# Padding the rows that expert lists gather from 260 to 272 numbers, in a graph-attention and mixture-of-experts kernel

## The chip, the core and the metric

The kernel runs on one core of one Trainium2 chip. The metric is the device time of one execution in microseconds (us); lower is better. The engines are PE (TensorE, matmuls; its weight loads are shown as PEld), DVE (VectorE), ACT (ScalarE), POOL (GpSimd) and SP (SyncE, which here only issues DMAs). Data moves by DMA between the device memory and the on-chip memory (128 partitions); matmul results land in PSUM.

## What is computed

One layer over 3327 nodes of 256 numbers: a graph attention over a sparse adjacency matrix, then a mixture of 16 experts, of which each node uses two.

```python
# graph attention, 4 heads of 64
h = (layernorm(x) @ W).reshape(n, 4, 64)
e = leaky_relu(einsum('nhd,d->nh', h, a1 + a2), 0.2)        # one score per node and head
attn = softmax(where(adj[:, None, :] > 0, e[:, :, None], -9e15), axis=-1)
x = x + layernorm(einsum('nhm,mhd->nhd', attn, h).reshape(n, 256)) * gamma + beta

# experts
xn = layernorm(x)
probs = softmax(xn @ gate_w + gate_b)
top_probs, top_idx = top_k(probs, 2); top_probs /= sum(top_probs)
hidden = silu(xn @ w1[e]) * (xn @ w2[e])                    # for every expert e
x = x + sum over the two chosen e of top_prob_e * (hidden @ w3[e])
```

## The kernel before

**Tiles and groups.** The 3327 nodes are padded to 26 tiles of 128. The tiles form seven groups (`SIZES`, line 68: 4, 4, 4, 4, 3, 4, 3). A group's rows lie on chip in one of the tiles of `XF` (line 259), 128 partitions by tiles of the group by `ROW` numbers, of which `X` is the first 256.

**Attention.** The adjacency matrix is loaded a group by a group at a time (L614), turned into a mask of zeros and ones by DVE (L617), and multiplied on PE with the nodes' values, split into a high and a low part (L640, L641). After each of the seven steps over rows, `finish` (line 664) turns a group's sums into its new rows: scaling by heads, two normalisations, the gate's logits, the choice of two experts.

**What is gathered later.** For each node `finish` makes a row of `ROW = D + 4 = 260` numbers in the tile `pay`: 256 normalised values (L765), two weights (L826, L827), and the numbers of the two experts (`chosen`, line 813; L816 writes the numbers, L817 and L819 make masks of them). SP stores a group's rows into the table `normed` in device memory (line 357, issued at L890). `places` (L833 to L837, PE) counts each node's place in its experts' lists, `placed`, `hot_rows`, `hot_pieces` (DVE), `coded` (ACT) and `listing` (PE, L874) write the lists.

**The experts.** There are 19 lists: experts 0 to 2 have an early list each, taken from groups 0 to 4 once these are done (`early_lists`, line 923), and a second one; the other 13 experts have one each, sorted by length (`all_lists`, line 935). `take_list` (line 1195) works a list off: 
- POOL gathers the rows of 128 nodes at a time from `normed` (`gather`, L1022; 61 instructions in all) into one of three buffers `XE`, which are the tiles `XF[0]`, `XF[1]` and `XF[5]`, free by then. Each indirect DMA reads whole rows of `ROW` numbers. Three lists' rows can thus be on chip or on their way at a time. 
- The rows are transposed, on PE (L1226) for lists 0 to 7 and by DMA transposes (L1180) for later ones. 
- The products with `w1` and `w2` (L1037 for lists 0 to 5; for later ones L1098, with seven products in place of eight, made by sums of blocks on DVE, L1070, and by copies between PSUM banks on ACT and DVE, L1104 and L1108), the gate (L1130, L1250) and the products with `w3` (L1151). 
- `weigh` (line 1025) picks each row's weight for this expert from its last four numbers (L1028, L1030). The results are scaled (L1274, L1276) and added into `out` by POOL's indirect DMAs (L1154).

**What sets the order.** From the first load to the last scatter-add, every piece of work is an entry in a `Plan` (class at the top of the kernel): engine, cost in us, rank, what it comes after, buffers. `best_order` tries 340 orders, in which the works of `finish` get small random delays; it simulates each with the entries' costs and sizes, and emits the one with the least simulated end. The emitted order is the order of each engine's queue. `chosen` is entered with a cost of 0.75 (`cho`, line 879), and the store with `size=n * P * ROW * 4` (L890).

**Constants.** At the start POOL fills tables, and clears what follows the 256 values in the three gather buffers (L352).

A few lines that the change touches:

```python
XF = [const.tile([P, len(tiles), ROW], F32, name=f"x{g}") for g, tiles in enumerate(GROUPS)]   # 259
XE = [XF[0], XF[1], XF[5]]                                                                     # 261
for xe in XE:                                                                                  # 351
    nc.gpsimd.memset(xe[:, :, D:], 0.0)
normed = tc.dram_tile([NP, ROW], F32, name="normed")                                           # 357
"pay": lambda key: work.tile([P, GT, ROW], F32, name="pay"),                                   # 421
```

Of the kernel before, what the change touches and what calls it, by code (L numbers as in the profile page):

```python
# [48 lines left out]
F32 = mybir.dt.float32  # L49
# [6 lines left out]
P = 128  # L56
# [3 lines left out]
D = 256  # L60
# [9 lines left out]
GROUPS = [list(range(sum(SIZES[:g]), sum(SIZES[:g + 1]))) for g in range(len(SIZES))]  # L70
# [21 lines left out]
PARTS = {m: 4 if m <= P // 4 else 2 if m <= P // 2 else 1 for m in range(1, P + 1)}  # L92

AGAIN = 2
ROW = D + 4
NONE = float(1 << 20)
I32 = mybir.dt.int32
U32 = mybir.dt.uint32
# [154 lines left out]
def gnn_moe(ctx: ExitStack, tc: tile.TileContext, x, adj_t, W, a, gamma, beta, gate_w, gate_b, w1, w2, w3, out):  # L253
    nc = tc.nc

    const = ctx.enter_context(tc.tile_pool(name="const", bufs=1))


    XF = [const.tile([P, len(tiles), ROW], F32, name=f"x{g}") for g, tiles in enumerate(GROUPS)]
    X = [t[:, :, :D] for t in XF]  # L260
    XE = [XF[0], XF[1], XF[5]]

# [93 lines left out]
    first_w3 = const.tile([P, JC * D], F32, name="first_w3")  # L356
    normed = tc.dram_tile([NP, ROW], F32, name="normed")

    WE = {}

    def load_weights(tiles, e, behind=()):

        at = bass.ds(e, 1)
        first = nc.sync.dma_start(tiles[0], w1[at].rearrange("o (k p) h -> p (o k) h", p=P))
        for other in behind:
            tc.add_manual_dep(first.ins, other.ins.name, mybir.DependencyInfo(
                mybir.DependencyClass.Sync, mybir.DependencyReason.DATA), reason="weights come behind these rows")
        nc.sync.dma_start(tiles[1], w2[at].rearrange("o (k p) h -> p (o k) h", p=P))
        nc.sync.dma_start(tiles[2], w3[at].rearrange("o (j p) d -> p (o j) d", p=P))

    def weight_tiles():
        up = POOLS["wmore"].tile([P, 2, KC, HID], F32, name="w12e")
        return [up[:, 0], up[:, 1], POOLS["wmore"].tile([P, JC, D], F32, name="w3e"), up]
# [13 lines left out]
    PE, DVE, ACT, POOL, SP = "PE", "DVE", "ACT", "POOL", "SP"  # L387
# [19 lines left out]
    def few_h(key):  # L407
# [12 lines left out]
        "w": lambda key: weight_tiles(),  # L420
        "pay": lambda key: work.tile([P, GT, ROW], F32, name="pay"),
        "xt": lambda key: work.tile([P, GT, KC, P], F32, name="xt"),
# [26 lines left out]
    plan = Plan(SLOTS, take)  # L449
# [10 lines left out]
    def by_tile(ap):  # L460
        return ap.rearrange("(t p) d -> p t d", p=P)
# [202 lines left out]
    def finish(g, terms, added, tables):  # L664
        tiles = GROUPS[g]
        n = len(tiles)
        late = int(g > EARLY_GROUP)
        ak, hk, pk, xk, ck = ("agg", g), ("hp", g), ("pay", g), ("xt", g), ("hc", g)
        rank = (3, g)

        fk = ("few", g)
# [7 lines left out]
        def pay():  # L679
            return T[pk]  # L680
# [4 lines left out]
        def some(name):  # L685
            return T[fk][name]
# [121 lines left out]
        def largest(t):  # L808
            best, who = some("best"), some("who")
            nc.vector.max(best[:, t, :], some("lg")[:, t, :])  # L810
            nc.vector.max_index(who[:, t, :], best[:, t, :], some("lg")[:, t, :])

        def chosen():
            names = pay()[:, :n, D + 2:D + 4]
            hot, both = some("hot"), some("both")
            nc.vector.tensor_copy(names, some("who")[:, :, :2])  # L816
            nc.vector.tensor_tensor(hot, number[:, None, None, :].to_broadcast([P, n, 2, NE]),  # L817
                                    names[:, :, :, None].to_broadcast([P, n, 2, NE]), op=ALU.is_equal)
            nc.vector.tensor_add(both, hot[:, :, 0, :], hot[:, :, 1, :])  # L819
# [51 lines left out]
        def listing():  # L871
# [4 lines left out]
        lk, ik = ("ph", "place", g), ("ph", "list", g)  # L876
        w = plan.add(DVE, 0.48, rank, gated + [root], biased, [gk, fk])
        top = [plan.add(DVE, 0.43, rank, [w], lambda t=t: largest(t), [fk]) for t in range(n)]
        cho = plan.add(DVE, 0.75, rank, top, chosen, [pk, fk])
        w = plan.add(DVE, 0.15, rank, top, lambda: nc.vector.tensor_sub(  # L880
            gap()[:, 0], some("best")[:, :, 1], some("best")[:, :, 0]), [fk])

# [2 lines left out]
        else:  # L885
# [4 lines left out]
        stored = plan.add(SP, 0.4, (2, g), [wei, cho] + xn, lambda: nc.sync.dma_start(  # L890
            by_tile(normed[tiles[0] * P:(tiles[-1] + 1) * P, :]), pay()[:, :n, :]), [pk], landing=1.8, size=n * P * ROW * 4)
        pla = plan.add(PE, 0.2, (0, g), [cho] + tables, places, [lk, fk], slack=slack)
# [132 lines left out]
    def weigh(weight, xe, tiles, name):  # L1025

        hit = small.tile([P, CT, 2], F32, name="hit")
        nc.vector.scalar_tensor_tensor(hit[:, :tiles], xe[:, :tiles, D + 2:], name, xe[:, :tiles, D:D + 2],  # L1028
                                       op0=ALU.is_equal, op1=ALU.mult)
        nc.vector.tensor_reduce(weight[:, :tiles], hit[:, :tiles], AX.X, ALU.add)  # L1030

# [163 lines left out]
    def take_list(i, indexed, stored, weights, opened, order):  # L1195
# [20 lines left out]
        def weighed():  # L1216
            weigh(T["weight", i], XE[i % 3], len(tiles), expert[:, i:i + 1])
# [97 lines left out]
    for step in range(NG):  # L1315
        if step + 1 < NG:
            g = step + 1
# [13 lines left out]
    for g in range(NG):  # L1331
        if g + 1 < NG:
            for step in range((g + 1) * NG, (g + 2) * NG):
                products(step, adjacency(step))
        s, c, l, d = finish(g, terms, add_beta(g, read[g]), tables)
        stored.append(s)
        spare.append(d)
        tables = [c]
        if g == EARLY_GROUP:
            i, c = early_lists(c, l)  # L1340
            tables = [c]
            ready.update({k: (i, list(stored)) for k in range(EARLY)})
        if g == NG - 1:
            i, ranked, o = all_lists(c, l)
            ready.update({k: (i, list(stored)) for k in range(EARLY, 2 * EARLY)})
            ready.update({k: (o, list(stored)) for k in range(2 * EARLY, NL)})
# [10 lines left out]
    def first_weights():  # L1357

        WE[0] = [at.rearrange("p (k m) -> p k m", k=k) for at, k in zip(
            [XF[g].rearrange("p t d -> p (t d)")[:, :KC * HID] for g in (2, 3)] + [first_w3], (KC, KC, JC))]  # L1360
        load_weights(WE[0], 0)
# [30 lines left out]
    with tc.If(many["value"] > 0):  # L1392
        with tc.For_i(0, NL) as i:
# [4 lines left out]
            with tc.For_i(0, full * (NT // AGAIN)) as c:  # L1398
# [3 lines left out]
                hit = small.tile([P, AGAIN, 2], F32, name="hit_again")  # L1402
# [7 lines left out]
                n = AGAIN * P  # L1410
# [53 lines left out]
```

## Time and profile before

| | us |
|---|---|
| median of 6 runs (513.77 to 516.5) | 514.48 |
| the profiled execution | 514.71 |
| its span, first to last instruction | 512.9 |
| PE busy | 495.0 |
| DVE busy | 343.9 |
| ACT busy | 247.3 |
| POOL busy | 215.6 |
| POOL in gathers (L1022), 61 instructions | 66.2 |
| POOL in scatter-adds (L1154), 61 instructions | 97.7 |

The mean granted clock of PE is 0.992 of full speed. A span is the time from the first instruction's start to the last one's end; the execution's time has 1.8 us more around it. A stretch's line gives, for each engine, the busy us and the number of instructions, then the granted clock, the mean busy share of the 16 DMA engines, and GB/s moved. A line of the order of time gives the start and the duration in us, the engine, the source line, the operation, and in brackets how long the engine was idle before it and what ended that. A line of waits gives who waited, for whom, us in total, how often, and the longest.

The gather's DMA queue (q0) also carries the scatter-adds: 13.75 MB of the 100.06 MB that the execution moves.

### The profile page before, as it was taken

The page shows a single profiled execution, that of the slowest core. Times are in us where ns is not written, and L with a number is a line of the kernel's source. Part 1 is how long each engine was busy: PE and PEld are TensorE (multiplying, and loading weights), DVE is VectorE, ACT ScalarE, POOL GpSimd, SP SyncE. Part 2 cuts the span into 40 slices and gives each one's busy share as a digit, 9 for nine tenths or more (in the row PEclk, how much of TensorE's full clock was granted, in tenths as well). Part 3 has the DMA queues.
Part 4 walks back from the last instruction along what each step waited for, and adds up shares of the span by engine and source line. Part 5 has one row for each costly group of instructions (what it writes and reads, how often), then busy time and mean ns, then how long its engine had stood idle before and what let it go on. Part 6 is the DMA issues. An engine that isn't in the chain of part 4 may idle for free. (4 is left out here: it accounts for less than half of the span.)

```text
span 512.9 us, 9578 instructions
## 1 busy us (share of the span) xinstructions
PE 495.0 (97%) x3239; PEld 447.0 (87%) x3240; DVE 343.9 (67%) x992; ACT 247.3 (48%) x679; POOL 215.6 (42%) x235
## 2 busy tenths in 40 slices
PE   8999999999999999999999996999999999999994
PEld 5889999999999999986778785988898999988983
DVE  5977563966859798678926486465567668777320
ACT  2661054456446844465322564555455556445441
POOL 5420021112022121746468665645855474543263
PEclk9999999999999999999999998999999999999998
DMA  8942979789779997474269765787877987682233
GB/s 258 365 159 66 316 239 304 240 276 303 235 248 314 358 333 250 128 262 104 64 154 329 223 140 95 138 167 176 175 129 183 220 238 152 85 251 23 25 41 38
DMA packets 85703, 100.06 MB, mean 195 GB/s; under 512 B 27150, under 2 KB 59154, under 8 KB 85652
## 3 DMA queue, kind: packets, MB, share of 16 engines
q1 hardware_dynamic: 74612, 85.42, 53.3%
q0 software_dynamic: 10768, 13.75, 17.4%
q8 instruction: 26, 0.43, 0.4%
q10 hardware_dynamic: 272, 0.26, 0.1%
q14 instruction: 25, 0.20, 0.1%
HBM read 81.55 MB, written 13.75 MB: 186 GB/s over the span
## 5 line engine op out<-in xcount | busy, mean ns | idle before, releaser
L640 PE MATMUL pa<-hi,mk 128*128 128x258 f32 x676 | 167.9, 289 | 0.0
L641 PE MATMUL pa<-lo,mk 128*128 128x256 f32 x676 | 163.4, 282 | 0.0
L1154 POOL DMA_INDIRECT out<-y,out_index x61 | 97.7, 1602 | 92.5 <-ACT y L1274 71.1
L640 PEld LDWEIGHTS pa<-hi,mk 128*128 128x128 f32 x676 | 127.9, 189 | 1.7 <-issue 1.6
L641 PEld LDWEIGHTS pa<-lo,mk 128*128 128x128 f32 x676 | 127.7, 189 | 0.1
L1151 PE MATMUL ph<-w3e,hid 128*128 128x256 f32 (+5 forms) x400 | 93.2, 385 | 0.0
L1151 PEld LDWEIGHTS ph<-w3e,hid 128*128 128x128 f32 (+5 forms) x400 | 75.3, 190 | 11.2 <-issue 0.7
L1022 POOL DMA_INDIRECT x<-normed,index x61 | 66.2, 1085 | 34.5 <-issue 13.3
L617 DVE TENSOR_SCALAR mk<-sg 128x2048 fp32r<-128x2048 f32 (+2 forms) x49 | 54.9, 1121 | 24.6 <-PE pa L641 23.6
L1130 ACT ACTIVATE s<-pa 128x256 f32<-128x256 f32 (+8 forms) x78 | 27.0, 346 | 43.8 <-PE pa L1098 25.7
L1098 PE MATMUL pt<-xt,w12e 128*128 128x256 f32 (+8 forms) x208 | 46.3, 347 | 1.3 <-DVE pa L1108 1.2
L706 POOL TENSOR_TENSOR hp<-csum,c 128x512 f32<-128x512 f32 x11 | 13.5, 1240 | 75.1 <-DVE c L702 56.5
L1274 ACT ACTIVATE y<-ph,weight 128x256 f32<-128x256 f32 (+4 forms) x50 | 23.6, 472 | 39.5 <-PE ph L1151 37.8
L1098 PEld LDWEIGHTS pt<-xt,w12e 128*128 128x128 f32 x208 | 36.1, 190 | 6.4 <-DVE pa L1108 2.5
L1133 DVE TENSOR_TENSOR hid<-s,pa 128x256 f32<-128x256 f32 (+8 forms) x78 | 28.9, 371 | 16.6 <-ACT s L1130 11.5
L1104 ACT COPY pa<-pt 128x512 f32<-128x512 f32 (+8 forms) x52 | 25.1, 498 | 18.6 <-PE pt L1098 11.8
L1108 DVE TENSOR_TENSOR pa<-pt,qs 128x512 f32<-128x512 f32 (+8 forms) x26 | 15.7, 604 | 23.0 <-PE pt L1098 20.5
L1108 DVE TENSOR_TENSOR c<-pt,qs 128x512 f32<-128x512 f32 (+8 forms) x26 | 15.5, 596 | 23.2 <-ACT pa L1104 17.9
L534 PE MATMUL ph<-w_sb,xnt 128*128 128x260 f32 x104 | 27.9, 409 | 0.0
L1098 PE MATMUL pa<-xsum,w12e 128*128 128x256 f32 (+8 forms) x104 | 23.3, 347 | 4.3 <-issue 4.3
L1037 PE MATMUL pa<-xt,w12e 128*128 128x352 f32 (+3 forms) x128 | 26.7, 360 | 0.0
L1098 PEld LDWEIGHTS pa<-xsum,w12e 128*128 128x128 f32 x104 | 18.1, 190 | 6.7 <-issue 5.2
(216 smaller groups left out, 833.0 us busy)
## 6 DMA issues: line engine op xcount, KB each, us to landing
sg<-in_adj_t SPq DMA_DIRECT2D x25, 1024.0 KB
sg<-in_adj_t SPq DMA_DIRECT2D x20, 768.0 KB
w12e<-in_ffn_w SPq DMA_DIRECT2D x30, 512.0 KB
w3e<-in_ffn_w SPq DMA_DIRECT2D x15, 512.0 KB
normed<-pay SPq DMA_DIRECT2D x5, 520.0 KB
out<-x SPq DMA_DIRECT2D x5, 512.0 KB
sg<-in_adj_t SPq DMA_DIRECT2D x4, 576.0 KB
x<-in_x SPq DMA_DIRECT2D x4, 512.0 KB
```

Source lines behind the costliest of these rows:

```text
L534: nc.tensor.matmul(ph[:, :H + D], T["xnt", g, t][:, k, :], w_sb[:, k, :], start=(k == 0), stop=(k == KC - 1))
L617: nc.vector.tensor_scalar(T[mk][:, :m, :n * P], T[sk][:, :m, :n * P], 0.0, None, op0=ALU.is_gt)
L640: nc.tensor.matmul(pa[:, :D + 2], lhs, HI[mg][:, i, H:], start=first, stop=False)
L641: nc.tensor.matmul(pa[:, :D], lhs, LO[mg][:, i, H:], start=False, stop=left[g, t] == 0)
L1022: return nc.gpsimd.indirect_dma_start(out=xe[:, t, :], out_offset=None, in_=normed[:limit], in_offset=at_rows(idx, t), bounds_check=limit ...
L1037: nc.tensor.matmul(p[:, :n], wt[:, k, j * P:(j + 1) * P], xt[:, k, :n], start=(k == 0), stop=(k == KC - 1))
L1098: nc.tensor.matmul(psum(key)[:, w * (CAP // 2):w * (CAP // 2) + half], lhs()[:, w, jp], rhs(), start=first and w == 0, stop=True, skip_gro ...
L1108: return plan.add(DVE, 0.16 + 1.02e-3 * n, (1, i, jp), after, lambda: nc.vector.tensor_tensor(dst(), both(psum(xx)), T[qs][:, :, :half], o ...
L1130: nc.scalar.activation(T[gk][:, t * half:(t + 1) * half], part(0), AF.Silu)
L1133: nc.vector.tensor_mul(T[hk][:, 2 * jp + j, t * half:(t + 1) * half], T[gk][:, t * half:(t + 1) * half], part(1))
L1151: nc.tensor.matmul(py[:m, :D], hid[:, j, t * P:t * P + m], w3e[:, j, :], start=(j == 0), stop=(j == JC - 1))
L1154: i = nc.gpsimd.indirect_dma_start(out=out, out_offset=at_rows(idx, t, m), in_=y[:m], in_offset=None, bounds_check=NP - 1, oob_is_err=Fals ...
```

## The change

`ROW` becomes `D + 16 = 272` numbers, 1088 bytes in place of 1040. The table `normed`, the tile `pay` and the three gather buffers take the new length; the tiles of the other four groups keep 260. The 12 added numbers of a row are set to zero in `pay` by DVE, for each group, and its work's cost in the plan goes from 0.75 to 0.82. `weigh` names its two numbers explicitly, so that the padding stays out. The clearing of the gather buffers (L352) now covers 16 numbers of each row, and the stores' sizes in the plan grow with `ROW`; both follow without an edit of their own.

```diff
-ROW = D + 4
+ROW = D + 16
...
-    XF = [const.tile([P, len(tiles), ROW], F32, name=f"x{g}") for g, tiles in enumerate(GROUPS)]
+    XF = [const.tile([P, len(tiles), ROW if g in (0, 1, 5) else D + 4], F32, name=f"x{g}") for g, tiles in enumerate(GROUPS)]
...
             names = pay()[:, :n, D + 2:D + 4]
             hot, both = some("hot"), some("both")
             nc.vector.tensor_copy(names, some("who")[:, :, :2])
+            nc.vector.memset(pay()[:, :n, D + 4:], 0.0)
             nc.vector.tensor_tensor(hot, number[:, None, None, :].to_broadcast([P, n, 2, NE]),
...
-        cho = plan.add(DVE, 0.75, rank, top, chosen, [pk, fk])
+        cho = plan.add(DVE, 0.82, rank, top, chosen, [pk, fk])
...
-        nc.vector.scalar_tensor_tensor(hit[:, :tiles], xe[:, :tiles, D + 2:], name, xe[:, :tiles, D:D + 2],
+        nc.vector.scalar_tensor_tensor(hit[:, :tiles], xe[:, :tiles, D + 2:D + 4], name, xe[:, :tiles, D:D + 2],
                                        op0=ALU.is_equal, op1=ALU.mult)
```

## The prediction

> **What bounds the kernel now.** I began with busy shares and the stretches of the span.
>
> ```profile
> PE 495.0 (97%) x3239; PEld 447.0 (87%) x3240; DVE 343.9 (67%) x992; ACT 247.3 (48%) x679; POOL 215.6 (42%) x235
> ```
>
> ```profile
> core 0: us, PE busy (x) PEld busy (x) DVE busy (x) ACT busy (x) POOL busy (x), PEclk, DMA share, GB/s
> 100.00:240.00 140.00, 138.91 (x1171) 131.13 (x1170) 108.47 (x375) 79.52 (x269) 41.53 (x48) 1.00 0.82 262
> 240.00:260.00 20.00, 19.96 (x92) 14.92 (x91) 15.39 (x60) 5.73 (x14) 9.90 (x8) 1.00 0.25 51
> 290.00:420.00 130.00, 124.22 (x624) 111.20 (x623) 84.70 (x192) 71.12 (x146) 76.53 (x60) 0.99 0.75 157
> 420.00:505.00 85.00, 84.89 (x487) 76.77 (x486) 51.11 (x124) 41.68 (x100) 38.57 (x25) 1.00 0.52 103
> ```
>
> PE is the bound in every stretch: in the attention (100 to 240 us), where the rows to be gathered are made, and through the experts' lists (from 240 us), where they are used. It starts at 1.27 us and its last matmul ends at 505.20 us; the 7.7 us after that are the last scatter-adds. Between the two it stands still for 8.7 us in 14 gaps. I read those next, from PE's waits and from the order of time.
>
> ```profile
> PE pa L1098 <- issue: 4.3, 1, 4.3
> PE pt L1226 <- ACT xt L1235: 0.5, 2, 0.2
> PE pt L1226 <- issue: 0.3, 1, 0.3
> ```
>
> ```profile
> 315.19 0.57 ACT L1104 COPY pa<-pt 128x512 f32<-128x512 f32 x1 [3.31 <-remote]
> 315.81 1.18 PE L1098 MATMUL pa<-xsum,w12e 128*128 128x256 f32 x4 [4.29 <-issue]
> ```
>
> ```profile
> 315.00:320.00 5.00, 4.19 (x12) 3.46 (x13) 4.12 (x9) 3.02 (x6) 1.83 (x2) 0.68 0.78 125
> ```
>
> Half of the standstill is one gap at 311.52 us. It costs 4.29 us, and then the granted clock falls to 0.68 over 5 us, another (1 - 0.68) x 5 = 1.6 us: 5.9 us in all. The trace names no releaser that I can follow to its cause. The other 13 gaps hold 8.74 - 4.29 = 4.45 us, 0.34 each. Only the three in front of L1226, the transposes of gathered rows, stand where a late gather could show: 0.24 + 0.25 + 0.34 = 0.83 us, and the waits above put 0.5 of it down to ACT.
>
> Last I asked who reads the gathered table and who waits for it.
>
> ```profile
> L1022 POOL DMA_INDIRECT x<-normed,index x61: 998/1031/1710, 205.7 to 418.5; - x61
> L890 SPq DMA_DIRECT2D normed<-pay x7: 372/383/384, 99.0 to 244.7; - x7
> ...
> who waited for it (us, times):
> busy tenths in 40 slices 0000000000000000520236463311301220000000
> ```
>
> The list under "who waited for it" is empty: no instruction's wait ended with a gather's landing. The last gather goes out at 418.5 us, 87 us before PE ends.
>
> **The change, part by part.** All sums are against the profiled execution: 514.71 us, of which the span is 512.9 and 1.8 lies around it. The median of the runs shown is 514.48, so 0.23 below.
>
> *Gathers (L1022).* 61 instructions as before, each 128 rows; POOL's 1031 ns makes the descriptors for 128 rows, and their number is the same. A row grows from 1040 to 1088 bytes. In the trace's packet records the gather queue (q0) moves four rows in one packet of 4160 bytes, 1658 of them, fastest tenth 160 ns, mean 273 ns, 28.3 us spread over 16 engines. So at best a row takes 40 ns at 1040 bytes and unaligned, while SP's plain packets of 1024 aligned bytes take 46 ns at the median and its stores of 1040 bytes 47. No penalty for crossing a 64-byte line is to be seen: there is none to win. Plain counting says the same: 1040 = 16.25 x 64, and a row that starts 0, 16, 32 or 48 bytes into a line always touches 17 lines; a padded row is 17 whole lines. Bounds: the padding costs 48/1040 = 4.6% of 28.3 us, +1.3 us, if all of it were on the path; if every packet fell to 160 ns, 113 ns x 1658 / 16 = 11.7 us of transfer time would go, but the path could take only the 0.83 us of L1226's gaps. So -0.8 to +1.3. I take 0: the cover is that rows are fetched at least a list ahead of PE. Without it, one gather is late by 4.6% of some 0.35 us (two packets per engine at 178 ns, the median), 16 ns.
>
> The Trainium skill, in "DMA: Bandwidth & Descriptors", section "How a descriptor splits into AXI transactions", speaks against the change: transactions begin at multiples of 256 bytes, whatever lies before the start is fetched too, and a beat is 32 bytes. By that rule, as an estimate, a 1040-byte row at the sixteen possible offsets takes 36.5 beats on the mean, and a 1088-byte row, which begins 0, 64, 128 or 192 bytes into 256, takes 37: the gathers would get 1.4% dearer instead of 4.6%, 0.4 us of transfer time in place of 1.3, and 0 on the path as above. A multiple of 64 isn't what that rule rewards. The 40 ns row of the trace doesn't contradict it, and tells no more.
>
> *Stores of normed (L890).* Seven, 520 to 544 KB for four tiles, 3328 rows x 48 bytes. Their packets are 10.2 us over 16 engines; +4.6% is 0.5 us in all, 0.07 each. The last ones, issued up to 244.7 us, are read first by gathers of lists 3 and on from 251.7 us, 7 us later. 0; uncovered at most +0.07 for the last. SP issues the same count of DMAs, and nothing is moved past another on a queue by hand.
>
> *Zeroing of the padding (L816 and after).* Seven new DVE memsets of 128 x 48 or 36 numbers. The rows next to it are memsets of 128x64 (0.11 us), 128x76 (0.12) and 128x4 (0.06): 7 x 0.06 to 0.12 = 0.4 to 0.8 us of DVE. Behind each stand L817, L819, then PE's placing (L833), the listing and the lists. Groups 0 to 3 are covered by the adjacency products. Groups 4 and 6 end in lists; after group 6, PE has the 28 matmuls of 7.42 us before it transposes list 3 at 260.39, and that list's gathers have gone out at 251.67 to 255.45. So 0 by cover; without it 2 x 0.12 = 0.24 us. I take 0.24, as DVE is 0.77 busy there (15.39 of 20 us) and delays on it collect.
>
> *POOL's clearing (L352).* Three memsets of 128x16 become 128x64: 101 ns each now, 0.19 for the three; a POOL memset of 128x128 takes 0.20 each. At most +0.3 us, at 3.56 us, in front of a POOL idle time of 0.58 us at 4.57. 0; uncovered +0.3.
>
> *The slices (L1028).* The same eight numbers per instruction, 220 ns. 0. *SBUF tiles:* 48 bytes more per tile of x0, x1, x5 and pay; instructions keep their shapes. 0.
>
> *The order.* This is the part that can cost or bring something. The instruction order on all five engines comes out of a search over orders that are ranked by simulated times. The choice's cost goes from 0.75 to 0.82 in seven works, and the stores' size grows with ROW; every later start in the search moves, so another of the tried orders can win, and then instructions after the first finish (94 us) stand differently. The trace can't price an order that it doesn't have. Bounds from this one: the long gap goes (-5.9 us), or a second one of its size comes (+5.9). Nearest is the kernel's own state, with the long gap kept. I add one more small gap, +0.34: the edits add work to DVE and DMA and take none away.
>
> Sum: 514.71 + 0 + 0 + 0.24 + 0 + 0.34 = 515.3 for a profiled execution, less 0.23 for the median: **515.1 us**.
>
> **The rivals.**
>
> *The order gets worse (slower).* A second standstill of the kind at 311.52 us arises in the lists, 290 to 505 us, where PE waits for ACT's and DVE's copies between products of the same pair (L1098, L1104, L1108). Price 4.29 + 1.6 = 5.9 us; half of it when the gap stays so short that the clock isn't lowered (the gaps of up to 0.62 us left it at 1.00). For it: after every such product PE has only four matmuls (1 us) before it needs the copy. Against: 420 to 505 us runs with 0.11 us of idle PE in the same code. 517 to 521 us. It decides from about 1 us of delay in one copy.
>
> *The order gets better (faster).* The long gap disappears: 515.1 - 5.9 = 509.2; with part of it left, up to 513. For it: it is one gap among 14, tied to what stands around it. Against: six runs within 513.8 to 516.5 around the profiled 514.71 suggest that it comes with this order each time, and a new order can bring its own.
>
> *Aligned gathers are faster after all, or do nothing.* If rows landed sooner, PE could gain L1226's 0.83 us: 513.9. Against it is the empty list of waiters. That alignment does nothing at all is in my forecast.
>
> **How the numbers follow.** A measurement of this kernel tells about 0.3% (1.54 us) from no change. My forecast, the long gap kept and a few small gaps more or less, 0.50, own range 512.5 to 517.0: same 0.30, slower 0.15, faster 0.05. Worse order 0.25, all slower. Better order 0.23, and gathers that gain beyond 0.3% through it 0.02, all faster. So faster 0.30, same 0.30, slower 0.40. The range reaches into both other cases until a tenth is left on each side: 509.5 to 520.5.
>
> **What would show it.** Right: L1022 at 1.03 us and still without waiters; q0's packets grown to 4352 bytes at 160 ns or a little above; seven DVE memsets of about 0.1 us; PE's busy time within 2 us of 495.0, and the difference of the spans equal to that of PE's gaps and of the time at lowered clock. Wrong: a wait that ends with normed or with a gather's landing; packets that hold three rows and cost more each; a last matmul at 505 us but a longer tail; matmuls that take longer at full clock.

## The result, and the profile after

The changed kernel takes 520.41 us (median of 25 runs, 515.44 to 525.12) against 515.46 us of the kernel before (51 runs, 511.67 to 522.33): ratio 1.0092, 95% interval 1.0071 to 1.0113, some 4.7 us slower (0.0092 x 515.46). The profiled execution took 519.01 us, its span 517.1. Ratios here and below leave out single executions more than 1.5% above the kernel's fastest; where medians of all runs say something else, they are given beside.

First the busy shares, and the same stretches as before; each stretch's line has the engines' busy us, the granted clock, the DMA share and GB/s.

```profile
PE 495.7 (96%) x3239; PEld 448.3 (87%) x3240; DVE 343.6 (66%) x999; ACT 248.1 (48%) x679; POOL 214.6 (41%) x235
```

```profile
100.00:240.00 140.00, 138.99 (x1174) 131.59 (x1172) 107.25 (x377) 78.26 (x266) 40.98 (x48) 1.00 0.81 263
240.00:260.00 20.00, 20.00 (x95) 15.23 (x94) 15.84 (x67) 7.39 (x17) 8.81 (x7) 1.00 0.27 53
260.00:290.00 30.00, 25.36 (x164) 21.66 (x163) 12.02 (x34) 6.26 (x22) 17.49 (x15) 0.94 0.73 245
290.00:420.00 130.00, 123.77 (x619) 110.05 (x618) 85.34 (x195) 71.09 (x144) 78.89 (x61) 0.99 0.76 158
420.00:509.00 89.00, 88.89 (x510) 80.84 (x509) 53.55 (x129) 43.98 (x106) 41.05 (x28) 1.00 0.53 113
```

PE is as full as before up to 260 us and from 420 us on. What is new lies in 260 to 290 us: 4.64 us without PE, and the clock down to 0.94. The kernel before had 1.59 us there, at full clock:

```profile
260.00:290.00 30.00, 28.41 (x185) 23.95 (x184) 14.37 (x42) 8.20 (x26) 21.99 (x19) 1.00 0.92 283
```

PE's waits name two long gaps where there was one, and a third of 1.6 us:

```profile
PE pa L1099 <- issue: 4.0, 2, 3.7
PE pa L1038 <- ACT s L1251: 3.9, 1, 3.9
PE pt L1099 <- ACT qs L1105: 1.6, 1, 1.6
```

In the order of time the two look like this (the changed kernel's lines are one further down than before's from line 817 on):

```profile
276.54 0.45 ACT L1251 ACTIVATE s<-pa 128x128 f32<-128x128 f32 x2 [5.95 <-remote]
276.85 0.48 DVE L1254 TENSOR_TENSOR hid<-s,pa 128x128 f32<-128x128 f32 x2 [2.63 <-ACT s L1251]
276.87 1.01 PE L1038 MATMUL pa<-xt,w12e 128*128 128x128 f32 x3 [3.92 <-ACT s L1251]
...
312.43 1.06 ACT L1105 COPY pa<-pt 128x512 f32<-128x512 f32 x2 [4.57 <-remote]
...
313.05 1.34 PE L1099 MATMUL pa<-xsum,w12e 128*128 128x256 f32 x4 [3.72 <-issue]
```

Both have the form of the one gap before: PE waits for ACT, and ACT for a matmul that by the records had been issued long ago ("remote": a release that fits no recorded instruction's end).

The account closes on PE. Start of PE 1.28 + busy 495.7 + gaps 12.37 + tail 7.68 = 517.0 us; before 1.28 + 495.0 + 8.74 + 7.68 = 512.7 us, both within 0.2 of the span. Of the 4.2 us between the spans, 3.63 are gaps and 0.7 is busy time. A stretch of 3.41 us at a granted clock of 0.50 comes with the end of each long gap; there was one before (from 316.76 us), and there are two now (from 276.29 and 313.84 us). The first of the two:

```profile
276.29:279.70 3.41, 2.83 (x13) 2.83 (x14) 1.73 (x5) 0.72 (x3) 0.00 (x0) 0.50 0.10 34
```

Who waits for the gathers, and what the new instructions cost:

```profile
L1023 POOL DMA_INDIRECT x<-normed,index x61: 992/1004/1622, 205.7 to 421.8; - x61
L891 SPq DMA_DIRECT2D normed<-pay x7: 372/383/556, 99.7 to 246.7; - x7
...
who waited for it (us, times):
busy tenths in 40 slices 0000000000000000420234453303320220000000
```

```profile
L817 DVE MEMSET pay<- x7: 88/98/98, 95.2 to 244.3; 128x48 f32 x5, 128x36 f32 x2
```

```profile
L352 POOL MEMSET x<- x3: 141/141/142, 3.6 to 3.7; 128x64 f32 x3
```

Still nobody waits for a gather. Its packets of four rows grew from 4160 to 4352 bytes, and their fastest tenth from 160 to 168 ns: 40 to 42 ns a row. The slower packets did not follow: the median fell from 178 to 168 ns, the mean from 273 to 267.

### The profile page after: what moved, and what is told of

The parts are those of the page before. It is cut to its first block, busy times and chain, and to the rows that moved or that the text cites. A ratio compares the mean times of both kernels' runs of the same rounds, so it can differ in the third digit from the quotient of the medians.

```text
span 517.1 us, 9593 instructions
## 1 busy us (share of the span) xinstructions
PE 495.7 (96%) x3239; PEld 448.3 (87%) x3240; DVE 343.6 (66%) x999; ACT 248.1 (48%) x679; POOL 214.6 (41%) x235
## 5 line engine op out<-in xcount | busy, mean ns | idle before, releaser
L1152 PE MATMUL ph<-w3e,hid 128*128 128x256 f32 (+5 forms) x400 | 91.5, 380 | 0.0
L1152 PEld LDWEIGHTS ph<-w3e,hid 128*128 128x128 f32 (+5 forms) x400 | 73.9, 187 | 10.4 <-issue 0.2
L617 DVE TENSOR_SCALAR mk<-sg 128x2048 fp32r<-128x2048 f32 (+2 forms) x49 | 53.8, 1098 | 29.6 <-PE pa L641 29.2
L1099 PE MATMUL pt<-xt,w12e 128*128 128x256 f32 (+8 forms) x208 | 46.0, 346 | 0.8 <-DVE pa L1109 0.7
L706 POOL TENSOR_TENSOR hp<-csum,c 128x512 f32<-128x512 f32 x11 | 12.3, 1129 | 76.5 <-DVE c L702 61.6
L1099 PEld LDWEIGHTS pt<-xt,w12e 128*128 128x128 f32 x208 | 36.1, 190 | 5.5 <-PE ph L1152 2.1
L1038 PE MATMUL pa<-xt,w12e 128*128 128x352 f32 (+3 forms) x128 | 28.2, 372 | 4.1 <-ACT s L1251 3.9
L1038 PEld LDWEIGHTS pa<-xt,w12e 128*128 128x128 f32 x128 | 20.9, 205 | 8.8 <-ACT s L1251 4.1
L1099 PE MATMUL pa<-xsum,w12e 128*128 128x256 f32 (+8 forms) x104 | 23.5, 348 | 4.0 <-issue 4.0
```

Of the source, the lines that this page charges most:

```text
L617: nc.vector.tensor_scalar(T[mk][:, :m, :n * P], T[sk][:, :m, :n * P], 0.0, None, op0=ALU.is_gt)
L1038: nc.tensor.matmul(p[:, :n], wt[:, k, j * P:(j + 1) * P], xt[:, k, :n], start=(k == 0), stop=(k == KC - 1))
L1099: nc.tensor.matmul(psum(key)[:, w * (CAP // 2):w * (CAP // 2) + half], lhs()[:, w, jp], rhs(), start=first and w == 0, stop=True, skip_gro ...
L1152: nc.tensor.matmul(py[:m, :D], hid[:, j, t * P:t * P + m], w3e[:, j, :], start=(j == 0), stop=(j == JC - 1))
```

## The experiments

The theory that I held: the order that the search deals makes the difference, rows and zeroing next to none. Its rival: the longer rows or the zeroing cost the time. Both halves of the change can be had alone, as the order depends only on what the plan is told.

**Order alone (e1), layout alone (e2).** PE's queue is the same, instruction for instruction, as the changed kernel's in e1 and as before's in e2.

```diff
# e1: kernel before, with the changed kernel's plan
-cho = plan.add(DVE, 0.75, ...          +cho = plan.add(DVE, 0.82, ...
-size=n * P * ROW * 4                   +size=n * P * (D + 16) * 4
# e2: changed kernel, with the old plan
-cho = plan.add(DVE, 0.82, ...          +cho = plan.add(DVE, 0.75, ...
-size=n * P * ROW * 4                   +size=n * P * (D + 4) * 4
```

> Rows of 260 and no zeroing, as before; the search over orders is given the changed kernel's numbers (choice 0.82, stores of 272), so that PE's queue is instruction for instruction that of the changed kernel. If the order makes the difference: ratio to before 1.006 to 1.012, PE standing still 11 to 14 us between its first and last matmul, with two gaps of 3.5 us or more near 273 and 309 us. If the longer rows or the zeroing make it: ratio 0.998 to 1.002 and one long gap as before.

> Rows of 272 and the zeroing, as changed; the search is given the old numbers (0.75, stores of 260), so that PE's queue is instruction for instruction that of before. If the order makes the difference: ratio 0.998 to 1.002, one long gap near 311 us. If the longer rows or the zeroing make it: ratio 1.006 to 1.012.

Measured, beside before's 519.98 us on that chip: e1 523.49 us, ratio 1.0038 (1.0004 to 1.0071; by the medians of all runs 1.0068); e2 517.60 us, ratio 0.9938 (0.9896 to 0.9979). The layout alone does not cost; it is even below before (by the medians of all runs 0.9954). The order alone does cost, though its ratio lies below the 1.006 that was expected at least. The profiles don't show the gaps that were expected: e1's has 1.68, 8.55 and 2.65 us at 276, 311 and 378 us, and e2's, in place of one long gap near 311 us, has several of 0.9 to 3.0 us between 268 and 381 us.

**Two other orders (e3, e4).** The search's random delays get another seed; rows of 260.

```diff
-        draw = random.Random(0)
+        draw = random.Random(1)      # e4: 2
```

> Nothing changed but the seed of the search's random delays (1 in place of 0): another of its orders, with rows of 260. If the order alone can move the time by as much as the change did: a ratio off 1 by 0.4% or more in either direction, carried by PE's long gaps. If orders of this search are all alike: 0.997 to 1.003.

> As with seed 1, with seed 2: a second draw. Order matters: off 1 by 0.4% or more, and not the same as seed 1. All alike: 0.997 to 1.003.

e3: 525.40 us, 1.0072 (1.0023 to 1.0120; by the medians of all runs 1.0104). e4: 518.20 us, 0.9977 (0.9937 to 1.0017), which is not told from 1, so that the 0.4% that was expected of it did not come. One of two other draws costs as much as the change did, with nothing else changed. It is less of a new draw than it seems: put side by side by line, tiles and shape, the traces of e3 and of the changed kernel have the same PE queue from 252 us on (from the 1918th of 3239 matmuls), and the same ACT queue. Where the gaps lie, e3 repeats the changed kernel's order on these two engines; e4's differs there from that one and from before's.

**The changed kernel and both halves on one chip (e5, e6, e7).** The kernels of the change, of e1 and of e2, on another chip than these.

> The changed kernel itself once more, beside the two halves on one chip. Both theories: 1.004 to 1.012. What counts is where it stands to the halves: if the order makes the difference, it goes with the kernel that has its order and rows of 260; if the layout does, with the one that has rows of 272 and the old order.

> The kernel of e1 again, beside the changed kernel. Order: within 0.4% of the changed kernel and 0.4 to 1.0% above before. Layout: at before's time, 0.997 to 1.003.

> The kernel of e2 again. Order: 0.993 to 1.002, and clearly below the changed kernel. Layout: with the changed kernel, 1.004 to 1.012. If the gain of e2 was chance: 0.998 to 1.002; if longer rows do bring something in the old order: 0.990 to 0.997 again.

| | rows of 260 | rows of 272, zeroed |
|---|---|---|
| old order | 520.27 us | e7: 518.67 us, 0.9894 (0.9825 to 0.9963) |
| new order | e6: 524.32 us, 1.0088 (1.0053 to 1.0124) | e5: 524.92 us, 1.0077 (1.0038 to 1.0116) |

With the new order the length of the rows makes no difference; the order makes one with either length. By the medians e7 is 0.3% below before; its low ratio, below all that was expected, rests on four executions. PE's waits in e6, which has the rows of before:

```profile
PE pa L1099 <- issue: 6.7, 2, 6.4
PE pt L1099 <- issue: 1.9, 1, 1.9
...
PE pa L1038 <- ACT xt L1236: 1.2, 1, 1.2
```

and in e5, the changed kernel:

```profile
PE pa L1099 <- issue: 7.4, 2, 7.1
PE pa L1038 <- ACT s L1251: 4.1, 1, 4.1
PE pt L1099 <- issue: 1.9, 1, 1.9
```

In these two and the first profile of the new order the gaps fall in the same three stretches: near 271 to 277 us (3.92, 4.08, and 1.20), 306 to 312 us (3.72, 7.06, 6.37) and 369 to 377 us (1.56, 1.93, 1.86). The second and the third stand before the same matmuls of PE's queue each time (the 2204th and the 2472nd), in e1 (8.55, 2.65) and in e3 (3.85, 1.97) too; the first stands before either of two matmuls. In the profile before, the gaps of the same stretches were 0.39, 4.29 and 0.62, and in e7, with the old order, 1.48, 4.35 and 0.54, the middle ones before other matmuls. So the order has a part in where PE stops, down to the matmul; the stretches are roughly the same in both orders, and the sizes change from one execution to the next.

In the profiled executions the time goes with PE's standstill between 205 and 430 us: 1.8 us at 503.81 us (e9, below), 8.1 at 514.71 (before), 12.5 at 518.68 (e6), 11.4 at 519.01 (the changed kernel), 17.4 at 525.35 (e5).

**Every gather twice (e8).** The kernel before, meant to double what a gather might disturb.

```diff
+gather(XE[i % 3], index_of(i), t, limit)
 GATHERED.setdefault(i, []).append(gather(XE[i % 3], index_of(i), t, limit))
```

> The kernel before, with every gather issued twice into the same rows (61 more POOL instructions of 1.03 us and 6.9 MB more); order, layout and results unchanged. This doubles the suspected disturbance: PE's long gaps stood only between 265 and 420 us, where POOL gathers, and ACT's waits there end late. If gathers under way are what makes PE stand still: PE's gaps between 265 and 430 us grow from 6 to 10 us to 12 us or more, ratio 1.01 or more. If gathers neither disturb nor are waited for: 0.997 to 1.003.

706.11 us, ratio 1.3579 (1.3481 to 1.3677): far beyond either theory, and for a reason that makes the test a failure as to disturbance. POOL's rows:

```profile
  DMA x<-normed,index: 157.5, 61
...
who waited for it (us, times):
  POOL x L1022: 157.5, 61
  ACT halves L1189: 112.3, 10
...
  PE pt L1226: 29.2, 7
...
DMA to landing us min/median/max: 2.4/2.9/7.1
```

The second gather writes the rows that the first one writes, so POOL waited 61 times for a landing, 157.5 / 61 = 2.6 us each, and ACT, DVE and PE then waited for rows. It shows that the cover of the gathers is finite: some 3 us more for each of the 61 tiles is more than it holds (186 us in all). Whether gathers under way hold PE up stays open.

**On a third chip: a control, the layout again, rows of 270, and a nudge (e9 to e12).** e9 is the kernel before itself; e10 is e2's kernel; e11 and e12 are

```diff
# e11: e2's kernel, 1080 bytes a row
-ROW = D + 16
+ROW = D + 14
# e12: kernel before
-cho = plan.add(DVE, 0.75, ...
+cho = plan.add(DVE, 0.76, ...
```

> The kernel before against itself, to see what a ratio of this size is worth here, where single runs of one kernel spread over some 2%. Ratio 0.996 to 1.004; if it is further off, the differences of the other runs are worth that much less.

> Rows of 272 with the old order, a third time, beside the control. If longer rows bring something in this order: 0.990 to 0.997, and below the control. If the two lower ratios so far were chance or single disturbed runs: 0.998 to 1.003.

> Rows of 270 numbers (1080 bytes, no multiple of 64) with zeroing and the old order. If beginning at a multiple of 64 bytes is what helps: at the control's time, above the rows of 272 by 0.4% or more. If alignment does nothing: the same as the rows of 272 within 0.4%, gather packets of four rows at about 40 ns a row in both.

> The kernel before with the choice's cost in the plan at 0.76 in place of 0.75 and nothing else: a nudge of 0.01 us in seven entries, which deals another order. If the order by itself moves the time: off the control by 0.4% or more in either direction. If orders near to each other are alike: within 0.3%.

| | us | ratio to before (503.95 us) |
|---|---|---|
| e9, before itself | 503.85 | 1.0000 (0.9984 to 1.0017) |
| e10, rows of 272 | 502.62 | 0.9978 (0.9961 to 0.9996) |
| e11, rows of 270 | 503.93 | 1.0001 (0.9987 to 1.0016) |
| e12, another order | 503.99 | 1.0009 (0.9993 to 1.0026) |

The same kernel takes 16 us less here than on the two chips of e1 to e8. The control's stretches and its PE waits:

```profile
260.00:290.00 30.00, 29.52 (x193) 25.40 (x193) 15.64 (x44) 9.25 (x27) 22.18 (x20) 1.00 0.92 288
290.00:420.00 130.00, 130.00 (x678) 118.46 (x677) 92.31 (x211) 76.52 (x156) 82.63 (x62) 1.00 0.78 176
```

```profile
PE pt L1226 <- ACT xt L1235: 0.7, 3, 0.2
PE pt L771 <- DVE x L755: 0.5, 1, 0.5
```

PE is busy for all of 290 to 420 us, and its gaps sum to 2.65 us over the whole span in place of 8.74. The long gaps are not there at all, and with them the effect of another order has gone (e12). By the traces e12's order is, on PE and ACT, that of the changed kernel and of e3 from 252 us on. In the stretch of the gaps, then, the order that went with 0.4% to 0.9% on the other chips goes with no cost here. The changed kernel itself was not run on this chip.

Rows of 272 come out below rows of 260 a third time (0.22%, between the two cases of the expectation), rows of 270 don't. The two differ by less than the 0.4% set down beforehand, their gather packets have medians of 168 and 167 ns, and PE's gaps are alike (2.71 us in e10, 2.65 in the control). So the multiple of 64 bytes is not shown to bring anything. The single profile of e10 is no help: its PE already leads the control by 1.6 us at its hundredth matmul (22.68 us against 24.28), before the first row is stored, and from 216 us to the end, where the gathered rows are used, the lead stays at 2.7 to 2.75 us. And PE reaches the matmul at L921 at 203.55 us in e10 and at 205.55 in the control, while in three other profiles with the same PE queue, before, e2 and e7, that matmul starts at 206.37, 206.35 and 206.51 us, rows of 260 or 272 alike. So the version with rows of 272 and the old order is below the kernel before in all three comparisons, by 0.2% to 1.1% (by the medians of all runs 0.3% to 0.5%), but what it owes that to isn't shown.

## Why the prediction was right, and where it was off

Slower was the likeliest of the three classes (0.40), and 520.41 us lies within 509.5 to 520.5, but only by 0.1 us, which is luck: the measured ratio alone is uncertain by 1 us either way. And the case that came is not the one the single figure was built on, 515.1 us: it is the rival "the order gets worse", 517 to 521 us. Point by point:

- *Gathers, 0.* Shown: no waiter; the layout alone never cost (e2, e7, e10). The packets grew by 5% in their fastest tenth (160 to 168 ns) for 4.6% more bytes. The rule of the Trainium skill ("DMA: Bandwidth & Descriptors", "How a descriptor splits into AXI transactions") would, by the prediction's estimate, have made it 1.4%; the fastest tenth goes with the bytes, and the median, 6% down from 178 to 168 ns, goes with neither. The prediction's "there is none to win" was read from the fastest tenth alone; something was won in the packets. It did not matter on the path. The cover named for the zero, rows fetched a list ahead, is real but less than the 3 us a tile of e8.
- *Stores, 0.* Nothing in the profile waits for them.
- *Zeroing, 0.24 us on the path, 7 x 0.06 to 0.12 of DVE.* Seven of 88 to 98 ns. e2, e7 and e10 show no cost of it on the path.
- *POOL's clearing, 0, at most +0.3.* 141 ns each in place of 101, 0.3 us for the three; covered.
- *The order, +0.34, bounds -5.9 to +5.9.* This is the term that was mis-sized: the change cost about 4.7 us, near the upper bound, and the order alone +2.0 (e1) to +4.6 us (e6) on the chips with long gaps. It leaves nothing for the rows (e6 1.0088 with the old rows, against e5 1.0077). I took the kernel's own state as the nearest row for an order that the trace doesn't have. The mechanism was in kind the one of the rival, more standstill of PE in long gaps with half-clock stretches behind them. In the result's profile and in e5 it is a second long gap (3.92 and 4.08 us); that one arose near 273 us (L1038, waiting for the gate on ACT), ahead of the stretch and not between products of a pair (L1099), where I had put it. In e6 it is one longer gap of 6.37 us, at L1099.
- *"It comes with this order each time".* Half wrong. The matmul before which PE stops mostly comes with the order, the size with the execution, and on the third chip the gaps of the old order don't come at all.
- *Rival "the order gets better".* Not seen for this change, and seed 2's 0.9977 isn't told from 1.

What stays open: what holds ACT's release back in a long gap; the trace names no instruction for it. On the first chips PE's gaps of 0.7 us or more lie between 268 and 382 us in every profile but e8's; on the third chip there are none.

## What to carry to other kernels

Where a search or a planner writes the instruction order, every edit of its inputs is two edits: the one meant, and a new draw. Give the edited kernel the old plan's numbers and the old kernel the new ones, on the same chip; four kernels tell which of the two moved the time. Compare the queues that come out as well: a new seed can deal the same order again in the stretch that matters. And a gap that the trace can't explain should be looked for on a second chip before anything is built on it: here gaps carried 3.63 of the 4.2 us, and on the third chip they were gone.

## What the runs showed of the hardware that was not expected

One kernel, without an edit, has medians of 515.46, 519.98, 520.27 and 503.95 us in four sessions, the last three on three different chips: 3% apart, where the change was 0.9%. The profiled difference (spans of 512.9 and 502.1 us) arises between 268 and 374 us. PE's queue is the same in both, and set side by side matmul by matmul the kernel is level with the control (e9) at 249 us (0.04 us), 10.7 us behind at 374 us, and no further behind at the end. Of this, 6.9 us are PE's gaps, 1.7 the half clock (3.41 us at 0.50), and the last 2 us lie in matmuls that follow each other more slowly, for which there is no account.

Crowded DMA engines don't tell the long gaps from the rest. At 310 to 315 us in the profile before, they were busy 0.32 of the time and moved 83 GB/s, while at 265 to 285 us, at a share of 1.03 and 330 GB/s, PE stood still for 1.0 us only. In the changed kernel's two long gaps the share was 0.84 and 0.91. There POOL's next gathers still go out, while PE does nothing and DVE and ACT hardly anything:

```profile
272.94:276.87 3.93, 0.01 (x1) 0.00 (x1) 0.50 (x2) 0.33 (x2) 1.99 (x2) 0.93 0.84 286
309.33:313.05 3.72, 0.00 (x2) 0.00 (x1) 0.02 (x1) 0.62 (x2) 2.81 (x4) 1.00 0.91 181
```
